# Two attention stages on one core: where the score maxima are subtracted, and when

## The chip, the cores and the metric

The kernel runs on one core of a Trainium2 chip. The metric is device time in microseconds (us), the median of the runs shown. A core has a matrix engine (PE, with its weight loads shown as PEld), a vector engine (DVE), an activation engine (ACT), GpSimd (POOL), and SyncE (SP), which here only issues DMAs. Each engine works through its own instructions in a fixed order; semaphores make one wait for another. PSUM is the memory into which PE writes.

## The reference

The input x is (8, 256, 512), cond is (8, 512), all float32. Four blocks are added to x one after the other. The change touches the first two, called here the masked and the modulated attention.

```python
# masked attention: x is (B, D, T), 8 heads of 32 channels, q = k = v
qh = (x^T @ Wq.T) in heads
logits = (scale * qh qh^T * cmask + (1 - cmask) * -1e30) * rmask
x = x + (softmax(logits) @ qh) @ Wo.T
# modulated attention: 16 heads of 32 channels
xn = rms_norm(x, g_norm) * (1 + scale) + shift     # scale, shift = cond @ W_emb + b_emb
q, k, v = xn @ W_qkv;  q = rms_norm(q, g_q);  k = rms_norm(k, g_k)
o = softmax(q k^T / sqrt(32)) @ v
x = x + o + o @ W_out
# then two scans over the 256 rows: an RK4 oscillator, and a GRU
```

## The kernel before

Attention and scans follow each other; the scans (from L540 on) keep eight batches together and walk through 256 steps. The attention part works on one batch at a time, with two stages interleaved by hand.

The order is written out: `for g in range(-5, ...)` walks over *slots*, and each slot calls small functions, each of which emits the instructions of one step. Instructions of one engine run in the order of these calls. Eight slots (`U = 8`) make a period, in which one batch passes through each step; `at(g, rel, n)` gives the batch and unit that a step serves in slot g. Below, "remainder r" means the slots with g mod 8 = r.

The masked stage has eight units per batch: two groups `e` of four heads, times four chunks `kc` of 128 keys. A unit is scored (`scores0`, L192) five slots before it is weighted (`weights0`, L224), and its values are summed (`values0`, L229) one slot later still. Scores are symmetric here, so the maximum over a row of a chunk (`maxima0`, L206) serves as maximum of a column. When the last chunk of a group is scored (remainders 3 and 7), `rows0` (L212) turns the maxima into a row, writes it to DRAM, and reads it back spread over 128 partitions into the tile `bc` (1 MB, one buffer). `weights0` subtracts `bc` on DVE (L226) from four heads' scores in SBUF, in one instruction of 128x2048, and ACT takes the exponential (L227). `weigh0` (remainders 1 and 5) divides on DVE, then masks and fills on POOL. `project`, `masked_out`, `normalize` and `modulate` come once or twice per period.

The modulated stage multiplies by `wqkv_sb` in six parts, one per slot (remainders 5, 6, 7, 0, 1, 2; two per slot for the last two batches). Of the q and k parts (remainders 7, 0, 1, 2) ACT makes squares and a copy, DVE sums (L326), POOL takes the power and scales (`qkv_norm`, L328 to L330), and one slot later PE transposes the result (`qkv_out`). Then come four groups `c` of four heads, one slot apart, from `HEADS[b]` on: `maxima1` in slot 0 of its own count, `rows1` and `weights1` in slot 1, `values1` in slot 2. `rows1` leaves the negative maxima as a row in SBUF; `weights1` forms the scores again with keys on the partitions and adds the row by a product with a column of ones (L384) into the same PSUM bank; ACT takes the exponential straight from PSUM.

All these steps take their PSUM banks from one pool of six, `ps_s`, in turn; a new bank waits until its last user, six banks ago, has been read. `values0` has two banks of its own, freed by `weigh0`.

At the end of slot 66 the masked stage's memory is closed and `follow()` issues the loads of the scan weights and of the transposed rows, all on SP (L535, L524), the queue which also carries the row and spread DMAs.

The names of the slots are those of the loop:

```python
            if a := at(g, 1, U):
                weights0(a[0], a[1] // 4, a[1] % 4)
...
            for part, lines in made:
                if lines:
                    qkv_norm(*part, *lines)
```

Of the kernel before, what the change touches and what calls it, by code (L numbers as in the profile page):

```python
# [14 lines left out]
P = 128  # L15
# [9 lines left out]
def attention(ctx, tc, cst, x, cond, wqT, woT, w_emb, b_emb, g_norm, w_qkv, g_q, g_k, w_out, follow):  # L25
# [53 lines left out]
    with tc.manual_schedule():  # L79
        nc.sync.dma_start(wq_sb, wqT.rearrange("(k p) e -> p k e", p=P))  # L80
        load(0)
        cst["rest"]()
        vec = wp.tile([12, P], F32, name="vec")
        nc.sync.dma_start(vec[0:8, :], b_emb.rearrange("(f p) -> f p", p=P))
        nc.sync.dma_start(vec[8:12, :], g_norm.rearrange("(f p) -> f p", p=P))
        gq_sb = wp.tile([P, 1], F32, name="gq_sb")
        gk_sb = wp.tile([P, 1], F32, name="gk_sb")
        for i in range(4):
            nc.sync.dma_start(gq_sb[32 * i : 32 * i + 32, :], g_q.unsqueeze(1))
            nc.sync.dma_start(gk_sb[32 * i : 32 * i + 32, :], g_k.unsqueeze(1))  # L90

        wemb = [
            two.tile([P, 2 * D], F32, tag=tag, name=f"wemb_{k}", bufs=bufs)
            for k, (tag, bufs) in enumerate((("qT", 1), ("kT", 1), ("vt", 2), ("vt", 2)))
        ]
        for k in range(NJ):
            nc.sync.dma_start(wemb[k], w_emb[k * P : (k + 1) * P, :])
        load(1)
        wo_sb = fone.tile([P, 2, 256], F32, name="wo_sb")
        nc.sync.dma_start(wo_sb, woT.rearrange("(k p) e -> p k e", p=P))  # L100
        wqkv_sb = wp.tile([P, NJ, 3 * D], F32, name="wqkv_sb")
        nc.sync.dma_start(wqkv_sb, w_qkv.rearrange("(k p) f -> p k f", p=P))
        wout_sb = wp.tile([P, NJ, D], F32, name="wout_sb")
        nc.sync.dma_start(wout_sb, w_out.rearrange("(k p) f -> p k f", p=P))

    gqs = wp.tile([P, 1], F32, name="gqs")
    mhalf = wp.tile([P, 16], F32, name="mhalf")
# [6 lines left out]
    mxp0 = [fone.tile([P, NJ, P], F32, name=f"mxp0_{i}") for i in range(2)]  # L114
    mxp1 = wp.tile([P, 2, P], F32, name="mxp1")
    for t in (*mxp0, mxp1):
# [6 lines left out]
    def modulation():  # L123

        nc.vector.tensor_scalar_mul(gqs, gq_sb, SC)
        pv = bank([P, 28], "pvs")
        nc.tensor.transpose(pv, cst["vecs"], ident[0:28, 0:28])
        nc.vector.tensor_copy(cst["vecS"], pv)
        pv = bank([P, 12], "pv")
        nc.tensor.transpose(pv, vec, ident[0:12, 0:12])  # L130
        nc.vector.tensor_copy(vecT, pv)
        pe = bank([P, 8, B], "pe")
        for f in range(8):
            for k in range(NJ):
                nc.tensor.matmul(
                    pe[:, f, :],
                    lhsT=wemb[k][:, f * P : (f + 1) * P],
                    rhs=condT[:, k, :],
                    start=(k == 0),
                    stop=(k == NJ - 1),  # L140
                )
# [3 lines left out]
        nc.vector.tensor_copy(shift, ssT[:, NJ:8, :])  # L145

        for c in range(NJ):
            nc.vector.tensor_add(wout_sb[:, c, c * P : (c + 1) * P], wout_sb[:, c, c * P : (c + 1) * P], ident)

# [19 lines left out]

    def project(b, e):  # L170
        if e == 0:
            qms[b] = ftwo.tile([P, 2, D], F32, tag="qm", name=f"qm_{b}")
# [6 lines left out]
        nc.vector.tensor_mul(qms[b][:, e, :], ps, mks[b])  # L179
# [11 lines left out]

    def scores0(b, e, kc):  # L192

        qm = qms[b]
        ss = [bank([P, D], f"s0_{b}_{e}_{kc}_{h}") for h in range(4)]
        for h in range(4):
            r = 32 * h
            nc.tensor.matmul(  # L198
                ss[h], lhsT=qm[r : r + 32, e, kc * P : (kc + 1) * P], rhs=qm[r : r + 32, e, :], start=True, stop=True
            )  # L200
        sc = ftwo.tile([P, 4, D], F32, tag="sc", name=f"sc_{b}_{e}_{kc}", bufs=7)
        for h in range(4):
            nc.scalar.copy(sc[:, h, :], ss[h])  # L203
        scs[b, e, kc] = sc

    def maxima0(b, e, qc):  # L206

        nc.vector.tensor_reduce(  # L208
            mxp0[e].rearrange("p q (h i) -> p q h i", i=32)[:, qc, :, 0], scs[b, e, qc], AX.X, ALU.max
        )  # L210

    def rows0(b, e):  # L212

        pt = bank([P, NJ, P], f"pm0_{b}_{e}")
        for qc in range(NJ):
            nc.tensor.transpose(pt[:, qc, :], mxp0[e][:, qc, :], ident)
        mrow = ftwo.tile([P, D], F32, tag="mrow", name=f"mrow0_{b}_{e}", bufs=1)
# [5 lines left out]

    def weights0(b, e, kc):  # L224
        sc = scs[b, e, kc]
        nc.vector.tensor_sub(sc, sc, bcs[b, e])  # L226
        nc.scalar.activation(sc, sc, AF.Exp, bias=negT[:, kc, b : b + 1], scale=SC)  # L227

    def values0(b, e, kc):  # L229
# [15 lines left out]

    def weigh0(b, e):

        fill = ftwo.tile([P, D], F32, tag="fill", name=f"fill_{b}_{e}", bufs=1)
        nc.gpsimd.tensor_scalar(fill, mks[b], -1.0, means[b, e], ALU.add, ALU.mult)
        cx = ctxTs[b][:, e, :]  # L250
        pv, pn = pc0s[b, e]
# [16 lines left out]
            nc.vector.tensor_add(xs[b][:, m, :], ps, xs[b][:, m, :])  # L268


    xhs, xnTs, qTs, kTs, vts, mrows1, exs1, oTs = {}, {}, {}, {}, {}, {}, {}, {}

    def normalize(b):
        ss = sm.tile([P, 2], F32, tag="ss", name=f"ss_{b}")
# [87 lines left out]
    def rows1(b, c):  # L362
        pt = bank([P, 2, P], f"pm1_{b}_{c}")
        for qc in range(2):
            nc.tensor.transpose(pt[:, qc, :], mxp1[:, qc, :], ident)
        mrows1[b, c] = two.tile([P, 256], F32, tag="mrow1", name=f"mrow1_{b}_{c}")
        nc.scalar.activation(mrows1[b, c], pt.rearrange("p q n -> p (q n)"), AF.Copy, scale=-1.0)

    def weights1(b, c):
        qT, kT, mrow = qTs[b], kTs[b], mrows1[b, c]  # L370
        ss = [bank([P, 2, 256], f"s1_{b}_{c}_{h}") for h in range(4)]
        for i in range(2):
            for h in range(4):
# [61 lines left out]
    for b in range(B):  # L435
# [26 lines left out]
    with tc.manual_schedule():  # L462
        for g in range(-5, OUT[-1][1] + 2):
# [549 lines left out]
```

## Time and profile before

| | |
|---|---|
| median of 3 runs | 2960.37 us (2959.13 to 2960.7) |
| the profiled execution, its own time | 2958.41 us |
| its span, from first to last instruction | 2956.6 us |
| mean granted clock of PE | 0.976 |
| PE, DVE, ACT, POOL busy, share of the span | 92%, 72%, 58%, 35% |
| first scan product (L709) on the chain of waits | 881.28 us |
| starts of slots 36, 44 and 52 (first `scores0` product) | 398.1, 497.1, 596.0 us |

The page's groups give for each line the engine, the operation, the tiles and shapes, the count, then busy time and mean length of one, then the idle time of the engine just before them and what ended it. A line of the timeline has the start in us, the length in us, the engine, the line and operation, and in brackets the wait before it. SPq is SyncE issuing DMAs; its length is the issue, not the transfer. A row of the windows has the stretch, its length, busy us and counts of PE, PEld, DVE, ACT, POOL, then the granted clock, the share of the DMA engines and GB/s. The spans of matmuls are modelled: where a matmul waits for a bank, its span may include the wait.

### The profile page before, as it was taken

To read this page: it belongs to the slowest core of one execution; us is meant where nothing else is said; L and a number is where in the kernel's file an instruction comes from. 1 tells how busy PE (TensorE), PEld (TensorE's weight loads), DVE (VectorE), ACT (ScalarE), POOL (GpSimd) and SP (SyncE) were. 2 spreads that over 40 slices of the span, in tenths; PEclk is the share of its full clock that TensorE was granted. 3 is DMA by queue.
4 is the path that set the end of the run, shared out by engine and by line. 5 is a ranking of instruction groups with operands and counts; after the bars stand their busy time and mean duration, and the time that the engine had idled before them with its cause. 6 is when DMAs were issued, how large, how long until landed. Compare 5 with 4: busy or idle time off the path is not lost.

```text
span 2956.6 us, 159809 instructions
## 1 busy us (share of the span) xinstructions
PE 2720.4 (92%) x67258; PEld 1930.5 (65%) x67258; DVE 2124.6 (72%) x8948; ACT 1720.9 (58%) x8427; POOL 1049.1 (35%) x2945
## 2 busy tenths in 40 slices
PE   6789999999988999999999999999999999999997
PEld 3234444444546777777777777777777777777776
DVE  4866676666446777777777777777777777777773
ACT  4655566554335666666666666666666666666551
POOL 0233123312313444444444444444444444444442
PEclk7989999999999999999999999999999999999998
DMA  3110101000600000000000000000000000000000
GB/s 143 40 40 29 40 26 47 29 33 23 129 15 4 7 6 7 6 7 7 7 6 7 6 7 7 6 6 7 7 7 7 6 7 7 6 7 6 6 7 6
DMA packets 27559, 57.60 MB, mean 19 GB/s; under 512 B 2816, under 2 KB 17164, under 8 KB 24788
## 3 DMA queue, kind: packets, MB, share of 16 engines
q1 hardware_dynamic: 26836, 47.36, 5.3%
q8 instruction: 526, 8.62, 1.2%
q14 instruction: 197, 1.61, 0.2%
HBM read 40.15 MB, written 7.21 MB: 16 GB/s over the span
## 4 chain that ended last, share of the span: by engine, by line
PE 39%; DVE 24%; ACT 5%; issue 3%; ACTq 0%; POOL 0%; DVEq 0%; POOLq 0%
PE pg L744 19%; PE ic L709 18%; DVE icT L901 5%; DVE qn L902 5%; ACT tT L609 4%; DVE hqs L862 3%; DVE own L759 3%; DVE sqmm L858 2%; DVE v L761 2%; DVE hz L789 2%; DVE own L778 1%; ACT sqmm L847 1%; DVE own L784 1%; PE psx L405 1%; ACTq L609 0%
## 5 line engine op out<-in xcount | busy, mean ns | idle before, releaser
L709 PE MATMUL ic<-cT_sb,tT 128*8 128x128 f32 x32736 | 1086.1, 273 | 82.3 <-ACT tT L609 45.6
L709 PEld LDWEIGHTS ic<-cT_sb,tT 128*8 128x8 f32 x32736 | 760.1, 89 | 339.8 <-ACT tT L609 268.5
L744 PE MATMUL pg<-whh_sb,hz 128*32 128x128 f32 x24576 | 820.9, 275 | 49.4 <-DVE hz L789 17.6
L609 ACT ACTIVATE tT<-qn 128x16 f32<-128x16 f32 x2046 | 440.8, 216 | 636.9 <-DVE qn L902 516.4
L744 PEld LDWEIGHTS pg<-whh_sb,hz 128*32 128x32 f32 x24576 | 669.5, 110 | 123.1 <-DVE hz L789 122.9
L901 DVE STREAM_TRANSPOSE icT<-ic 128x64 f32<-128x64 f32 x2048 | 504.2, 246 | 67.6 <-PE ic L709 63.2
L902 DVE SCALAR_TENSOR_TENSOR qn<-icT,hqs 128x16 f32<-128x16 f32 x2048 | 350.7, 171 | 70.1
L704 POOL TENSOR_TENSOR W<-W,cx 128x128 f32<-128x128 f32 x765 | 297.3, 389 | 256.6 <-ACT cx L690 256.4
L697 POOL TENSOR_TENSOR W<-cx,us 128x128 f32<-128x128 f32 x255 | 116.9, 458 | 445.0 <-ACT cx L690 445.0
L858 DVE SCALAR_TENSOR_TENSOR sqmm<-sqmm,qn 128x32 f32<-128x32 f32 x768 | 153.5, 200 | 151.4 <-ACT sqmm L847 122.4
L862 DVE TENSOR_TENSOR hqs<-W,sqmm 128x32 f32<-128x32 f32 x1020 | 199.9, 196 | 46.1 <-DVE own L784 1.0
L723 PE MATMUL gi<-wih_sb,x3T 128*32 128x384 f32 (+2 forms) x3072 | 201.5, 379 | 0.5 <-POOL x3T L914 0.5
L690 ACT ACTIVATE cx<-qn 128x32 f32<-128x32 f32 x1280 | 200.9, 213 | 0.0
L227 ACT ACTIVATE sc<-sc,negT 128x2048 f32<-128x2048 f32 x64 | 128.6, 2010 | 89.2 <-DVE sc L226 79.2
L305 PE MATMUL psqkv<-wqkv_sb,xnT 128*128 128x512 f32 x384 | 174.8, 600 | 0.2 <-DVE oT L165 0.2
L690 ACT ACTIVATE cx<-p 128x32 f32<-128x32 f32 x1020 | 149.8, 217 | 32.4 <-DVE p L857 1.6
L226 DVE TENSOR_TENSOR sc<-sc,bc 128x2048 f32<-128x2048 f32 x64 | 147.8, 2310 | 11.9 <-DMA bc<-row 11.9
L203 ACT COPY sc<-s 128x512 f32<-128x512 f32 x256 | 132.1, 617 | 40.6 <-PE s L198 40.4
L759 DVE STREAM_TRANSPOSE own<-pg 128x128 f32<-128x128 f32 x256 | 84.8, 331 | 94.8 <-PE pg L744 94.8
L208 DVE TENSOR_REDUCE mxp<-sc 128x4 f32<-128x2048 f32 x64 | 145.8, 2279 | 6.7 <-ACT sc L203 6.7
L690 ACT ACTIVATE cx<-q 128x32 f32<-128x32 f32 x1020 | 145.5, 213 | 0.0
L847 ACT ACTIVATE sqmm<-qn 128x32 f32<-128x32 f32 x768 | 140.5, 183 | 0.6
(149 smaller groups left out, 3364.0 us busy)
## 6 DMA issues: line engine op xcount, KB each, us to landing
bc<-row SPq DMA_DIRECT2D x16, 1024.0 KB
x<-in_x SPq DMA_DIRECT2D x8, 512.0 KB
out<-o SPq DMA_DIRECT2D x256, 16.0 KB
wqkv_sb<-in_L_cond_W_qkv SPq DMA_DIRECT2D x1, 3072.0 KB
wih_sb<-in_L_cond_W_ih SPq DMA_DIRECT2D x4, 768.0 KB
whh_sb<-in_L_cond_W_hh SPq DMA_DIRECT2D x4, 768.0 KB
x2d<-x2o SPq DMA_DIRECT2D x11, 256.0 KB
x2T<-x2d SPq DMA_DIRECT2D x11, 256.0 KB
```

Source lines behind the costliest of these rows:

```text
L305: nc.tensor.matmul(ps, lhsT=xnTs[b][:, c, m * P : (m + 1) * P], rhs=wqkv_sb[:, c, part * D : (part + 1) * D], start=(c == 0), stop=(c == N ...
L609: nc.scalar.activation(tT, src[:, half * HM : (half + 1) * HM, :], AF.Tanh)
L690: nc.scalar.activation(c[:, i], x, AF.Copy, scale=f)
L704: nc.gpsimd.tensor_tensor(W[:, i + 1 : 5], W[:, i + 1 : 5], c, ALU.add)
L709: nc.tensor.matmul(ps[32 * j : 32 * j + B, :], lhsT=tT[k // HM][:, k % HM, :], rhs=cT_sb[:, k, j * P : (j + 1) * P], start=(k == 0), stop= ...
L723: nc.tensor.matmul(gi_ps[rows(j), g0:g1, :], lhsT=x3T[c][:, k, :], rhs=wih_sb[:, k, g0:g1, j * P : (j + 1) * P], start=(k == 0), stop=(k = ...
L744: nc.tensor.matmul(pg_ps[rows(j), :], lhsT=hzs[tau % 3][:, k, 32 * g : 32 * g + 32], rhs=whh_sb[:, k, g, j * P : (j + 1) * P], start=((k, ...
L759: nc.vector.transpose(pgt.rearrange("p m n -> p (m n)"), pg_ps)
L858: stt(mm, sq, LIN[s], qs, ALU.subtract, ALU.mult)
L862: nc.vector.tensor_sub(hq, W[:, s], mm)
L901: nc.vector.transpose(icT.rearrange("p m n -> p (m n)"), ic[:, half * 64 : half * 64 + 64])
L902: stt(qn[:, m2, :], icT[:, :, 0:B], IC[s], hq[:, m2, :], ALU.mult, ALU.add)
```

## The change

- `weights0` subtracts on GpSimd (POOL) instead of DVE.
- `rows1` writes the maxima to DRAM and reads them back spread over 128 partitions (`bc1`, 512 KB, two buffers). `weights1` drops the product with ones; DVE subtracts `bc1` from the scores in PSUM, ACT takes the exponential of the result in SBUF.
- The heads' steps lie one slot further apart from their maxima: `weights1` two slots after `maxima1`, `values1` three. Within a slot both stand ahead of `qkv_out` and `qkv_norm`. `modulated_out` comes 8 and 9 slots after `HEADS[b]` instead of 6 and 8 (7 and 8 instead of 6 and 7 for the last two batches), so the loop has one slot more.
- `rows0` stands right behind the last `maxima0` instead of at the slot's end. There is one `mxp0` tile instead of two; `mrow` and `fill` share a buffer; `qm` is one tile per head group.
- `modulation()` runs in slot 1 instead of 4; the identity is added to `wout_sb` in slot 8; `w_qkv` and `w_out` are loaded at the end of slot -1 instead of ahead of the loop.

```diff
-        wqkv_sb = wp.tile([P, NJ, 3 * D], F32, name="wqkv_sb")
+    wqkv_sb = wp.tile([P, NJ, 3 * D], F32, name="wqkv_sb")
+    wout_sb = wp.tile([P, NJ, D], F32, name="wout_sb")
+
+    def load_weights():
+
         nc.sync.dma_start(wqkv_sb, w_qkv.rearrange("(k p) f -> p k f", p=P))
-        wout_sb = wp.tile([P, NJ, D], F32, name="wout_sb")
         nc.sync.dma_start(wout_sb, w_out.rearrange("(k p) f -> p k f", p=P))
...
     def weights0(b, e, kc):
         sc = scs[b, e, kc]
-        nc.vector.tensor_sub(sc, sc, bcs[b, e])
+        nc.gpsimd.tensor_tensor(sc, sc, bcs[b, e], ALU.subtract)
         nc.scalar.activation(sc, sc, AF.Exp, bias=negT[:, kc, b : b + 1], scale=SC)
...
-        mrows1[b, c] = two.tile([P, 256], F32, tag="mrow1", name=f"mrow1_{b}_{c}")
-        nc.scalar.activation(mrows1[b, c], pt.rearrange("p q n -> p (q n)"), AF.Copy, scale=-1.0)
+        mrow = two.tile([P, 256], F32, tag="mrow1", name=f"mrow1_{b}_{c}")
+        nc.scalar.copy(mrow, pt.rearrange("p q n -> p (q n)"))
+        row = dram.tile([4, 256], F32, tag="row1", name=f"row1_{b}_{c}", bufs=2)
+        nc.sync.dma_start(row, mrow.rearrange("(h i) n -> h i n", i=32)[:, 0, :])
+        bc = bcs1[b, c] = two.tile([P, 4, 256], F32, tag="bc1", name=f"bc1_{b}_{c}")
+        nc.sync.dma_start(bc, row.rearrange("h n -> (h n)").partition_broadcast(P).rearrange("p (h n) -> p h n", h=4))
...
                     start=True,
-                    stop=False,
-                )
-            for h in range(4):
-                r = 32 * h
-                nc.tensor.matmul(
-                    ss[h][:, i, :], lhsT=ones[r : r + 1, :], rhs=mrow[r : r + 1, :], start=False, stop=True
+                    stop=True,
                 )
...
             ex = sm.tile([P, 2, 256], F32, tag="ex1", name=f"ex1_{b}_{c}_{h}", bufs=4)
-            nc.scalar.activation(ex, ss[h], AF.Exp)
+            nc.vector.tensor_sub(ex, ss[h], bc[:, h, :].unsqueeze(1).to_broadcast([P, 2, 256]))
+            nc.scalar.activation(ex, ex, AF.Exp)
...
-        OUT.append((HEADS[b] + 6, HEADS[b] + (8 if per == 1 else 7)))
+        OUT.append((HEADS[b] + (8 if per == 1 else 7), HEADS[b] + (9 if per == 1 else 8)))
...
-            if g == 4:
+            if g == 1:
                 modulation()
+            if g == U:
+                add_identity()
...
-            for a in leave("qkv"):
-                qkv_out(*a)
             for b in range(B):
                 if g in OUT[b]:
                     m = OUT[b].index(g)
                     left["x2", b, m] = modulated_out(b, m)
+
+            if a := heads(g, 3):
+                values1(*a)
+            if a := heads(g, 2):
+                weights1(*a)
+            for a in leave("qkv"):
+                qkv_out(*a)
...
             if last:
                 maxima0(a[0], a[1] // 4, 3)
+                rows0(a[0], a[1] // 4)
             if a1:
                 maxima1(*a1)
-            if a2 := heads(g, 2):
-                values1(*a2)
-            if a2 := heads(g, 1):
-                weights1(*a2)
             if a and not last:
                 maxima0(a[0], a[1] // 4, a[1] % 4)
-            if last:
-                rows0(a[0], a[1] // 4)
             if (a2 := at(g, -7)) and a2[0] > 1:
                 load(a2[0])
+            if g == -1:
+                load_weights()
```

More of the change, by code (lines that the diff above doesn't have):

```diff
@@ L113, in attention @@
     nc.vector.tensor_scalar(negT, condT, NEG, -NEG, ALU.mult, ALU.add)
-    mxp0 = [fone.tile([P, NJ, P], F32, name=f"mxp0_{i}") for i in range(2)]
+    mxp0 = fone.tile([P, NJ, P], F32, name="mxp0")
     mxp1 = wp.tile([P, 2, P], F32, name="mxp1")
-    for t in (*mxp0, mxp1):
+    for t in (mxp0, mxp1):
         nc.vector.memset(t, 0.0)
@@ L145, in modulation, with add_identity @@
         nc.vector.tensor_copy(shift, ssT[:, NJ:8, :])
+    def add_identity():
         for c in range(NJ):
@@ L171, in project @@
         if e == 0:
-            qms[b] = ftwo.tile([P, 2, D], F32, tag="qm", name=f"qm_{b}")
             qtoks[b] = ftwo.tile([P, NJ, 256], F32, tag="qtok", name=f"qtok_{b}")
@@ L178, in project @@
             )
-        nc.vector.tensor_mul(qms[b][:, e, :], ps, mks[b])
+        qms[b, e] = ftwo.tile([P, D], F32, tag="qm", name=f"qm_{b}_{e}", bufs=3)
+        nc.vector.tensor_mul(qms[b, e], ps, mks[b])
         qt = line(f"qt_{b}_{e}")
@@ L192, in scores0 @@
     def scores0(b, e, kc):
-        qm = qms[b]
+        qm = qms[b, e]
         ss = [bank([P, D], f"s0_{b}_{e}_{kc}_{h}") for h in range(4)]
@@ L198, in scores0 @@
             nc.tensor.matmul(
-                ss[h], lhsT=qm[r : r + 32, e, kc * P : (kc + 1) * P], rhs=qm[r : r + 32, e, :], start=True, stop=True
+                ss[h], lhsT=qm[r : r + 32, kc * P : (kc + 1) * P], rhs=qm[r : r + 32, :], start=True, stop=True
             )
@@ L208, in maxima0 @@
         nc.vector.tensor_reduce(
-            mxp0[e].rearrange("p q (h i) -> p q h i", i=32)[:, qc, :, 0], scs[b, e, qc], AX.X, ALU.max
+            mxp0.rearrange("p q (h i) -> p q h i", i=32)[:, qc, :, 0], scs[b, e, qc], AX.X, ALU.max
         )
@@ L215, in rows0 @@
         for qc in range(NJ):
-            nc.tensor.transpose(pt[:, qc, :], mxp0[e][:, qc, :], ident)
-        mrow = ftwo.tile([P, D], F32, tag="mrow", name=f"mrow0_{b}_{e}", bufs=1)
+            nc.tensor.transpose(pt[:, qc, :], mxp0[:, qc, :], ident)
+        mrow = ftwo.tile([P, D], F32, tag="row", name=f"mrow0_{b}_{e}", bufs=1)
         nc.scalar.copy(mrow, pt.rearrange("p q n -> p (q n)"))
@@ L246, in weigh0 @@
     def weigh0(b, e):
-        fill = ftwo.tile([P, D], F32, tag="fill", name=f"fill_{b}_{e}", bufs=1)
+        fill = ftwo.tile([P, D], F32, tag="row", name=f"fill_{b}_{e}", bufs=1)
         nc.gpsimd.tensor_scalar(fill, mks[b], -1.0, means[b, e], ALU.add, ALU.mult)
@@ L268, in masked_out @@
             nc.vector.tensor_add(xs[b][:, m, :], ps, xs[b][:, m, :])
-    xhs, xnTs, qTs, kTs, vts, mrows1, exs1, oTs = {}, {}, {}, {}, {}, {}, {}, {}
+    xhs, xnTs, qTs, kTs, vts, bcs1, exs1, oTs = {}, {}, {}, {}, {}, {}, {}, {}
     def normalize(b):
@@ L365, in rows1 @@
             nc.tensor.transpose(pt[:, qc, :], mxp1[:, qc, :], ident)
-        mrows1[b, c] = two.tile([P, 256], F32, tag="mrow1", name=f"mrow1_{b}_{c}")
-        nc.scalar.activation(mrows1[b, c], pt.rearrange("p q n -> p (q n)"), AF.Copy, scale=-1.0)
+        mrow = two.tile([P, 256], F32, tag="mrow1", name=f"mrow1_{b}_{c}")
[4 more added lines that the diff above has]
+        nc.sync.dma_start(bc, row.rearrange("h n -> (h n)").partition_broadcast(P).rearrange("p (h n) -> p h n", h=4))
     def weights1(b, c):
-        qT, kT, mrow = qTs[b], kTs[b], mrows1[b, c]
+        qT, kT, bc = qTs[b], kTs[b], bcs1[b, c]
         ss = [bank([P, 2, 256], f"s1_{b}_{c}_{h}") for h in range(4)]
```

## The prediction, written before the changed kernel ran

> **What bounds the kernel now.** I read the page first, then the chain of waits, the windows of the attention stage, its timeline slot by slot, and at the end SyncE's own timeline.
>
> ```profile
> PE 2720.4 (92%) x67258; PEld 1930.5 (65%) x67258; DVE 2124.6 (72%) x8948; ACT 1720.9 (58%) x8427; POOL 1049.1 (35%) x2945
> ...
> PE pg L744 19%; PE ic L709 18%; DVE icT L901 5%; DVE qn L902 5%; ACT tT L609 4%; DVE hqs L862 3%; DVE own L759 3%; DVE sqmm L858 2%; DVE v L761 2%; DVE hz L789 2%; DVE own L778 1%; ACT sqmm L847 1%; DVE own L784 1%; PE psx L405 1%; ACTq L609 0%
> ...
> L226 DVE TENSOR_TENSOR sc<-sc,bc 128x2048 f32<-128x2048 f32 x64 | 147.8, 2310 | 11.9 <-DMA bc<-row 11.9
> ...
> L704 POOL TENSOR_TENSOR W<-W,cx 128x128 f32<-128x128 f32 x765 | 297.3, 389 | 256.6 <-ACT cx L690 256.4
> ```
>
> The chain is nearly all scan (L709, L744). The scans start at 881 us and are not touched, so the change moves the time by what it does to the 881 us before them. There eight slots make a period of 99 us (slot 36 starts at 398.1, slot 44 at 497.1, slot 52 at 596.0).
>
> ```profile
> 400.00:450.00 50.00, 48.62 (x421) 24.88 (x420) 35.75 (x32) 28.87 (x49) 6.19 (x6) 0.97 0.09 27
> 450.00:500.00 50.00, 46.10 (x244) 18.11 (x245) 33.75 (x29) 29.89 (x49) 19.18 (x17) 0.97 0.13 43
> ```
>
> The columns are PE, PEld, DVE, ACT, POOL busy, clock, DMA. PE looks 95% busy, but that hides waits inside a matmul's span: eight L198 stream in 0.86 us when free, yet take 2.1 to 3.3 us where they wait for PSUM banks. Added up from free-running rows (0.43 us for a 128x512 pass), a period holds 78 us of PE work of 99. So the stage is bound by hand-overs in the fixed order of each engine, not by one engine's work. The timeline of slot 39 (it starts at 437.73) shows the one that matters:
>
> ```profile
> 446.39 0.69 DVE L326 TENSOR_REDUCE s<-sq 128x16 f32<-128x512 f32 x1 [3.28 <-ACT sq L318]
> ...
> 447.17 0.20 POOL L328 TENSOR_SCALAR r<-s 128x16 f32<-128x16 f32 x1 [25.78 <-DVE s L326]
> 447.46 2.93 POOL L329 TENSOR_TENSOR r<-r,mhalf 128x16 f32<-128x16 f32 x1
> ...
> 450.47 1.05 POOL L330 TENSOR_TENSOR qr<-qr,r 128x512 f32<-128x512 f32 x1
> ```
>
> POOL needs 4.4 us (447.17 to 451.52) for one q/k normalisation, in four slots of eight (remainders 7, 0, 1, 2), and nothing else stands behind it there.
>
> **POOL subtraction.** 64 DVE subtractions of 2.31 us go (147.8 us), 64 POOL ones come. Price: POOL two-input rows are 389 ns at 128x128 (L704) and 1274 ns at 128x512 (L257), so 2.305 ns a column and 1274 + 1536 x 2.305 = 4.81 us. Low end 4 x 1.05 = 4.2 us (L330, one input repeated); high end 6.7 us, from a POOL fill that took 2.60 instead of 0.69 us beside DVE. I take 4.81, nearest to L257. POOL rises by 308 us, to some 64 us of a period: enough room.
>
> The Trainium skill ("GPSIMD Engine Reference", the elementwise comparison) speaks against this step: it gives 4497 ns on GpSimd and 2293 ns on VectorE for a two-input add of this width; with its figure the loop below would be 0.3 us shorter per slot.
>
> Does DVE hold POOL up? It does today:
>
> ```profile
> 178.49 2.28 DVE L226 TENSOR_TENSOR sc<-sc,bc 128x2048 f32<-128x2048 f32 x1
> 178.60 2.24 POOL L328 TENSOR_SCALAR r<-s 128x16 f32<-128x16 f32 x1
> ```
>
> A 0.20 us instruction lasts until L226 ends. L226 is the only DVE operation of the stage with both inputs in SBUF, and it goes; beside PSUM-reading L410 (472.96) POOL's L257 kept its 1.28 us. So no surcharge.
>
> **What queues behind it.** In each slot the exponential of the masked scores (L227, 2.0 us) waits for the subtraction, and behind it on ACT stand that slot's L318/L320, the modulated exponentials, L344 and the next score copies. On POOL the subtraction of slot g+1 stands behind the normalisation of slot g, which needs DVE's sum L326, which needs ACT's L318 of slot g, which stands behind the exponential of slot g. That closes a loop in the normalising slots: normalise 4.4 + subtract 4.85 + exponential 2.05 + square 0.6 + sum 0.75 = 12.65 us per slot. In between slots POOL runs ahead, so remainder 7 enters free. Counted from its start to the start of remainder 4:
> - sum of squares done after 14.4 us: scores with bank waits 1.9, values 1.7, q/k products 3.4, `values1` 1.8, DVE reciprocal and multiply 2.2, four new subtractions 2.75, sum 0.7 (before: 447.08 - 437.73 = 9.4, since the sum came ahead of these);
> - to the next sum 16.2: PE meets `rows0` right behind `maxima0` of DVE and stands until 17.2, then 7.8 us to the end of `values1` and 5.65 us of DVE;
> - two loops, 25.3; the last normalisation 4.4;
> - remainder 3: subtract 4.85, exponential 2.05, L182 0.8, squares 1.6, scale 1.0, L282 1.4, L344 0.7, `maxima1` 0.9 = 13.3.
>
> Sum 73.6 us against 497.07 - 437.73 = 59.3: +14. The other three slots (39.6 us) lose about 2 us by the part below. So +12 a period, for five periods (slots 20 to 60) **+60 us**. My same hand sum for the old order gives 90 of its 99 us, so +20 is possible; if POOL ran further ahead than I see, +4. The first batch alone (slots 15 to 20, no heads): first sum at 7.4, then 37.9 + 4.4 + 13.3 = 63 against 199.8 - 145.7 = 54.1, **+9** (4 to 12). The two doubled slots of batch 6, two normalisations (8.7) ahead of the last subtraction: **+8** (0 to 12).
>
> **Maxima spread by DRAM.** Gone: the L384 products, 0.43 us for four heads, twice for each of 32 groups, 28 us of PE, and PE's wait for L367 in the same slot. Where the loop bounds, that buys nothing; elsewhere it is the 2 us above. New: 128 DVE subtractions of 128x512 from PSUM at 0.69 (L410), 88 us, and 32 row writes and 512 KB spreads on SP. A row lands in 1.75 us (452.40 to 454.14); a 1 MB spread takes 4.7 us, so 3.5 for half (2.4 to 4.7). A slot covers that in the middle. At the end nothing does: copy 0.4, row 1.75, spread 3.5, subtract and exponential 3.3 make 9 us per group against 6.0 to 6.6 (`values1` at 854.62, 860.87, 866.92), three times and a partly covered first: +10. The last batch's sums now stand behind reciprocals and subtractions, +9; its output product moves out of their way, -4. **+15** (5 to 22).
>
> **SP's queue.** The scan loads are issued at the end of slot 66; `rows1` of batch 6, groups 1 to 3, come behind them.
>
> ```profile
> 770.07 1.82 SPq L535 DMA_DIRECT2D cT_sb<-in_L_cond_coupling  x4
> ...
> 773.91 3.31 SPq L535 DMA_DIRECT2D whh_sb<-in_L_cond_W_hh  x4
> 781.49 31.99 SPq L524 DMA_DIRECT2D x2T<-x2d  x11
> ```
> ```profile
> 796.00:800.00 4.00, 4.00 (x18) 1.86 (x21) 0.00 (x0) 1.13 (x3) 0.00 (x0) 1.00 1.03 218
> ```
>
> SP is occupied until 813.5, and the DMA share stays at 1.0 until 817. Group 1's spread then lands near 821; its subtractions, in slot 68, would be due at 803. DVE waits, behind it the maxima of group 3, which hold PE's banks: **+19** (5 to 25).
>
> **Start.** Today 4 MB of weights stand ahead of the first row:
>
> ```profile
> 32.99 0.35 SPq L222 DMA_DIRECT2D bc<-row  x1
> 37.72 2.29 DVE L226 TENSOR_TENSOR sc<-sc,bc 128x2048 f32<-128x2048 f32 x1 [7.33 <-DMA bc<-row]
> ...
> 42.16 1.94 PE L238 MATMUL pc<-sc,qtok 128*32 128x512 f32 x8 [10.98 <-ACT sc L227]
> ...
> 59.37 6.97 PE L135 MATMUL pe<-condT,wemb 128*128 128x8 f32 x47
> ```
>
> With the weights behind it the row (24.63) lands at 26.4 and the spread at 31.1, 6.6 us earlier. The modulation's 10.5 us of PE (59.4 to 69.9) fall into the 11 us in which PE waits; without that cover they would cost what they cost now. DVE's maxima of unit 5 queue behind them until about 38, and ran at 39.9 before. Then POOL sets the pace: four subtractions 19.3, the single `bc` buffer refilled 4.7, fill and two context steps 3.2, 27.2 us for four slots against 26 (L226 of unit 4 at 73.67, unit 8 at 99.47). Subtractions begin 18.6, 17 and 24 us earlier (units 4, 8, 12) and last 2.5 longer: **-18** (-12 to -22). The identity add (0.9 us) and shared row buffers cost nothing: their users are two slots apart.
>
> **Sum.** -18 + 9 + 60 + 8 + 19 + 15 = +93. The profiled run has its own 2958.41 us (span 2956.6), 1.96 under the median of 2960.37; 2958.4 + 93 + 2 = 3053 us. All low ends together give +12 (2972), all high ends +159 (3119).
>
> **Rivals.**
> - Faster (0.11): PE's order is what ends last and the loop is covered. For: PE shows 95%, the loop closes only in four slots. Against: PE waits of 21 us a period. Price: the period scales with PE work, 78.2 less 3.5 for L384, 99 x 74.7/78.2 = 94.6, so -4.4, five times -22, start -18, tail and SP +10: 2930. It decides if the ACT exponential finds its input ready in remainders 0 to 3, which needs a POOL subtraction of about 2 us, or a loop below the 10.5 us that slots 40 to 42 take now.
> - Loop hidden, but SP jam and tail in full (0.04): -40 + 34, 2955, no change.
> - POOL is also blocked by DVE's PSUM-reading work (0.05): 6.7 us each, 1.9 more in four links, 7.6 a period, five times +38: 3091, and more where the first batch and the start feel it too.
>
> The Trainium skill ("SBUF — State Buffer", the shared port pair) says a DVE instruction with two SBUF inputs excludes a GpSimd one that reads SBUF; the two rows at 178.5 agree. By that page this last rival would not happen.
>
> **How the numbers follow.** My forecast has 0.80, and 3053 is its time. The range 2970 to 3110 reaches from all low ends to near all high ends, takes in most of the third rival, and leaves out the faster one and the upper tail. A measurement of this kernel can tell about 0.2% (6 us) from no change. Faster 0.11, same 0.03, slower 0.86.
>
> **What would show it.** Right: POOL subtraction near 4.8 us x64; in remainders 0 to 3 ACT's exponential waiting for POOL by 5 us and more; a period near 111 us; DVE waiting for the modulated spread once for some 15 us near the scan loads; the first masked values near 38. Wrong: a period of 99 or less, that exponential never waiting, or that spread arriving ahead of the scan loads.

## The result, and the profile after

The changed kernel takes 3143.44 us (median of 4 runs, 3140.49 to 3145.13) against 2960.14 us for the kernel before (4 runs, 2959.13 to 2960.7): 1.062 times as long, 95% interval 1.0603 to 1.0637, +183 us. Predicted were 3053 us (+93) and at most 3110: the sign was right, the size half of what came; even all high ends of the prediction's terms together (3119) lie below the result. The profiled execution of after took 3144.8 us.

| stretch, from the starts of the slots | before | after | difference | predicted |
|---|---|---|---|---|
| start to slot 20 | 199.8 | 203.5 | +4 | -9 (-18 and +9) |
| slots 20 to 52, four periods | 396.2 | 490.2 | +94 | +48 |
| slot 52 to the end, a period more, batches 6 and 7 | 2362.4 | 2451.1 | +89 | +54 (12, 8, 19, 15) |

These are the two profiled executions, 3144.8 less 2958.4 = +186.

Line numbers are those of each kernel's own file: in the changed one `weights0` is L232 and L233, `values0` L244, `qkv` L311, `qkv_norm` L332 to L336, `maxima1` L358 and L366, `weights1` L385 to L396, the reciprocal behind `values1` L170, the scan loads L545 and L534.

The page after, first the engines, then groups as explained above (busy and mean, then the idle time of the engine just before them):

```profile
PE 2801.5 (89%) x66746; PEld 1935.9 (62%) x66746; DVE 2067.1 (66%) x9011; ACT 1731.5 (55%) x8427; POOL 1324.2 (42%) x3009
...
L232 POOL TENSOR_TENSOR sc<-sc,bc 128x2048 f32<-128x2048 f32 x64 | 289.0, 4524 | 28.7 <-DMA bc<-row 28.7
...
L233 ACT ACTIVATE sc<-sc,negT 128x2048 f32<-128x2048 f32 x64 | 128.5, 2008 | 180.9 <-POOL sc L232 180.8
...
L396 ACT ACTIVATE ex<-ex 128x512 f32<-128x512 f32 x128 | 77.5, 630 | 147.9 <-DVE ex L395 147.9
```

PE is busy 81 us longer for 512 matmuls fewer. ACT's masked exponential (L233) now waits 180.9 us for POOL, ACT's modulated one (L396) 147.9 us for DVE. The windows of one period, slots 36 to 44 (PE, PEld, DVE, ACT, POOL busy, granted clock, DMA share, GB/s), of after and then of before:

```profile
447.97:569.79 121.82, 106.92 (x589) 44.21 (x585) 61.03 (x66) 59.60 (x94) 60.33 (x31) 0.86 0.13 46
```
```profile
398.11:497.07 98.96, 93.67 (x649) 42.66 (x648) 68.46 (x59) 57.73 (x94) 25.37 (x22) 0.97 0.11 36
```

121.8 us instead of 99.0, DVE and POOL each only half busy, and PE's clock at 0.86 instead of 0.97. Slot 39 of after (490.34 to 511.52), which the prediction followed, and the beginning of slot 40:

```profile
493.74 1.94 PE L244 MATMUL pc<-sc,qtok 128*32 128x512 f32 x8
...
497.31 4.42 PE L311 MATMUL psqkv<-wqkv_sb,xnT 128*128 128x512 f32 x8
...
503.66 1.76 DVE L170 RECIPROCAL r<-pc 128x256 f32<-128x256 f32 x1 [8.49 <-PE pc L160]
...
505.80 2.47 DVE L395 TENSOR_TENSOR ex<-s,bc 128x512 f32<-128x512 f32 x4
...
508.19 0.68 DVE L332 TENSOR_REDUCE s<-sq 128x16 f32<-128x512 f32 x1
...
508.95 0.20 POOL L334 TENSOR_SCALAR r<-s 128x16 f32<-128x16 f32 x1 [25.04 <-DVE s L332]
...
511.12 0.47 PE L222 MATMUL pm<-ident,mxp 128*128 128x128 f32 x1 [4.57 <-DVE mxp L214]
...
513.26 4.53 POOL L232 TENSOR_TENSOR sc<-sc,bc 128x2048 f32<-128x2048 f32 x1
...
517.83 2.00 ACT L233 ACTIVATE sc<-sc,negT 128x2048 f32<-128x2048 f32 x1 [2.14 <-POOL sc L232]
```

Read down: the sum L332 stands behind reciprocal and four subtractions on DVE, POOL waits 25 us for it, its masked subtraction stands behind the normalisation, and ACT waits for that. In slots 40 to 43 that last wait is 2.1, 6.3, 7.9 and 6.6 us. So the loop is there. What the prediction had too small comes before it: the first sum ends 18.5 us into slot 39, not 14.4.

### The profile page after: what moved, and what is told of

It reads as the page before. It is cut to its first block, busy times and chain, and to the rows that moved or that the text cites. A ratio compares the mean times of both kernels' runs of the same rounds, so it can differ in the third digit from the quotient of the medians.

```text
span 3143.0 us, 159050 instructions
## 1 busy us (share of the span) xinstructions
PE 2801.5 (89%) x66746; PEld 1935.9 (62%) x66746; DVE 2067.1 (66%) x9011; ACT 1731.5 (55%) x8427; POOL 1324.2 (42%) x3009
## 4 chain that ended last, share of the span: by engine, by line
PE 53%; DVE 26%; ACT 7%; POOL 6%; issue 4%; DMA 2%; SPq 1%; ACTq 0%; DVEq 0%; POOLq 0%
PE pg L754 18%; PE ic L719 16%; DVE icT L911 5%; DVE qn L912 4%; PE psqkv L311 4%; ACT tT L619 4%; PE pc L244 4%; DVE hqs L872 3%; POOL sc L232 3%; PE s L204 3%; DVE own L769 3%; DVE sqmm L868 2%; DVE v L771 2%; PE n L358 2%; POOL r L335 2%
## 5 line engine op out<-in xcount | busy, mean ns | idle before, releaser
L232 POOL TENSOR_TENSOR sc<-sc,bc 128x2048 f32<-128x2048 f32 x64 | 289.0, 4524 | 28.7 <-DMA bc<-row 28.7
L233 ACT ACTIVATE sc<-sc,negT 128x2048 f32<-128x2048 f32 x64 | 128.5, 2008 | 180.9 <-POOL sc L232 180.8
L311 PE MATMUL psqkv<-wqkv_sb,xnT 128*128 128x512 f32 x384 | 180.0, 615 | 1.0 <-DVE oT L171 1.0
L170 DVE RECIPROCAL r<-pc 128x256 f32<-128x256 f32 x32 | 56.2, 1758 | 186.5 <-PE pc L160 186.5
L396 ACT ACTIVATE ex<-ex 128x512 f32<-128x512 f32 x128 | 77.5, 630 | 147.9 <-DVE ex L395 147.9
L204 PE MATMUL s<-qm 32*128 32x512 f32 x512 | 143.1, 798 | 14.6 <-ACT qr L326 8.9
```

What stands on the lines that cost most here:

```text
L204: nc.tensor.matmul(ss[h], lhsT=qm[r : r + 32, kc * P : (kc + 1) * P], rhs=qm[r : r + 32, :], start=True, stop=True)
L232: nc.gpsimd.tensor_tensor(sc, sc, bcs[b, e], ALU.subtract)
L311: nc.tensor.matmul(ps, lhsT=xnTs[b][:, c, m * P : (m + 1) * P], rhs=wqkv_sb[:, c, part * D : (part + 1) * D], start=(c == 0), stop=(c == N ...
```

## The experiments

Each run has its ratio to the kernel before with a 95% interval. A period is read from the starts of the slots, as above.

### Which part costs what: two switches

**e1: masked subtraction back on DVE.**
```diff
-        nc.gpsimd.tensor_tensor(sc, sc, bcs[b, e], ALU.subtract)
+        nc.vector.tensor_sub(sc, sc, bcs[b, e])
```


> The changed kernel with one line put back: the masked maxima are subtracted on DVE again. Loop theory (subtraction behind normalisation on POOL, exponential behind the subtraction on ACT, squares behind the exponential, closes a ring): the stretch from a remainder-7 slot to the next remainder 4, 79.5 us in the changed kernel, falls to about 60, the period from 122 to about 101, the time to 3143 - 5 x 21 - 15 = about 3025. Rival, order and banks (modulated scores now wait in PSUM for DVE, the maxima of the next group stand right behind them and wait for the same banks, PE's granted clock sinks to 0.8): with 2.3 us more on DVE in each slot the period stays at 115 or more, the time at 3110 or more.

3083.57 us, ratio 1.0412 (1.0385 to 1.0439): 60 us less than the changed kernel, between the two expectations. Periods are 112.6 to 116 us. Two thirds of the loss have nothing to do with POOL.

**e9: e1, without the subtraction of the modulated maxima.**
```diff
-            nc.vector.tensor_sub(ex, ss[h], bc[:, h, :].unsqueeze(1).to_broadcast([P, 2, 256]))
-            nc.scalar.activation(ex, ex, AF.Exp)
+            nc.scalar.activation(ex, ss[h], AF.Exp)
```


> The changed kernel with the subtraction back on DVE, and without the subtraction of the modulated maxima (left out; ACT takes the exponential straight from PSUM, the spread is made and not read). It takes 88 us of DVE work away and leaves the order as it is. If these instructions on DVE's queue are the price of the new order: period 100 to 104, and no DVE wait for the spread at the scan loads, 3000 to 3025 us. If the order costs by itself: period 110 or more, only the wait at the scan loads goes (some 28 us), 3050 to 3060 us.

2965.38 us, ratio 1.0034 (1.0017 to 1.0051), lower than either expected. What is left of the change here (new order, longer distance, start moves, 64 more DMAs, no products with ones) costs 0.3% net; taking 128 DVE instructions of 0.68 us (79 us of busy time, since they overlap a little) out of e1 buys 118 us. Not all of that lies in the periods. From the traces of e1 and e9: 51 us between slots 20 and 52, 20 from there to the first product of batch 6's maxima, 35 from that one to batch 7's (the stretch of the scan loads, where DVE in e1 waits for a spread that e9 does not read), 12 behind, and 4 the other way at the start.

**e11: the changed kernel, POOL and all, with the same edit as e9.**

> The changed kernel with its subtraction on GpSimd, without the subtraction of the modulated maxima (left out; exponential straight from PSUM). It asks whether the two costs add. If they do: 3143 less 118 (what these instructions cost with the masked subtraction on DVE) is 3025 us, or 2965 plus the 44 that GpSimd's subtraction cost in the kernel before, 3010 us: 3005 to 3030 us, periods 107 to 112. Rival: GpSimd's loop paces the slots by itself, so that leaving out DVE work buys little: above 3070 us, periods 116 and more.

3015.62 us, ratio 1.0194 (1.0179 to 1.0209), as expected if the costs add. With the changed kernel this makes a square:

| time in us (slots 36 to 44, granted clock there) | masked subtraction on DVE | on POOL | POOL costs |
|---|---|---|---|
| modulated maxima not subtracted | 2965 (102.5, 0.93) | 3016 (109.3, 0.94) | +50 |
| subtracted on DVE from PSUM | 3084 (112.6, 0.89) | 3143 (121.8, 0.86) | +60 |
| the subtractions cost | +118 | +128 | |

**e2: the kernel before, with only the masked subtraction on POOL.**

> The kernel before with one line changed: the masked maxima are subtracted on POOL. Loop theory: three loops of about 12.4 us (subtraction 4.52 as measured) enter the stretch from remainder 7 to remainder 4, first sum at 9.4 as before: 9.4 + 37 + 4.4 + 12.4 = 63 against 59.3, so +4 a period, +20 in five, +8 in the first batch and the start a few us slower, about 2990 to 3010. Rival, order and banks: DVE is freed of 2.3 us a slot and nothing else moves, 2950 to 2965.

3003.42 us, ratio 1.0148 (1.0128 to 1.0167), +44: 19 us by slot 20, then 6 to 8 us in each period (105 to 107 us). The loop theory's range held it.

### Is POOL's price the loop?

**e3: the changed kernel with `qkv_norm` ahead of the heads' steps.** DVE's sum L332 comes ahead of reciprocal and subtractions.
```diff
+            turned = list(leave("qkv"))
+            for part, lines in made:
+                if lines:
+                    qkv_norm(*part, *lines)
+                    left["qkv", *part] = lines[1]
             if a := heads(g, 3):
                 values1(*a)
             if a := heads(g, 2):
                 weights1(*a)
-            for a in leave("qkv"):
+            for a in turned:
                 qkv_out(*a)
-            for part, lines in made:
...
```


> The changed kernel with the q/k sums and normalisation called ahead of values1 and weights1 in each slot, so that DVE sums before it divides and subtracts. Loop theory with its place of entry: the first sum is done about 8 us sooner after the slot begins (18.5 to about 10.5), the second link falls from 18.6 to about 13, 13 us a period, time about 3143 - 65 = 3075. Rival, order and banks: the sums are not on the path, 3130 to 3150.

3093.23 us, ratio 1.0456 (1.0437 to 1.0475), -50, where 68 had been expected. Between 195 and 700 us ACT's masked exponential waits 62 us for POOL, in the changed kernel 96.

**e14: the same move, with the masked subtraction on DVE.**

> The changed kernel with the masked subtraction back on DVE (3083.6 us) and the normalisation of q and k ahead of the heads' values and weights. On the changed kernel itself that move alone bought 50 us. If it did so by shortening GpSimd's loop, it is worth within 12 us of nothing here: 3072 to 3096 us. Rival: it did so by moving DVE's sum ahead of the reciprocal and the new subtractions, whoever subtracts the masked maxima: 3030 to 3050 us.

3092.2 us, ratio 1.0446 (1.0431 to 1.0462), +9 against e1 (the granted clock in slots 36 to 44 is 0.83 here, 0.89 in e1; why, was not followed). With the sum ahead, POOL and DVE as subtracter differ by 1 us (ratios 1.0456 and 1.0446), with the sum behind by 60. So POOL's price is the loop (subtraction behind normalisation, sum behind subtractions, square behind exponential), not its 4.5 us as such; that PE's slower rows hide a part of it in e3 and e14 is not excluded.

### Why do the subtractions from PSUM cost more than they last?

The same slot (38) in e1 and in e9, here from the products of `weights1` on. e1:

```profile
463.72 1.15 PE L385 MATMUL s<-qT,kT 32*128 32x256 f32 x16
463.86 1.76 DVE L170 RECIPROCAL r<-pc 128x256 f32<-128x256 f32 x1 [6.47 <-PE pc L160]
...
465.99 2.47 DVE L395 TENSOR_TENSOR ex<-s,bc 128x512 f32<-128x512 f32 x4
466.22 2.61 PE L358 MATMUL n<-kT,qT 32*128 32x256 f32 x15 [0.99 <-DVE oT L171]
...
468.67 2.48 DVE L366 TENSOR_REDUCE mxp<-n 128x2 f32<-128x512 f32 x4 [0.21 <-PE n L358]
...
472.01 1.94 PE L244 MATMUL pc<-sc,qtok 128*32 128x512 f32 x8
```

e9, where ACT empties the banks of `weights1` itself:

```profile
434.79 1.15 PE L385 MATMUL s<-qT,kT 32*128 32x256 f32 x16
...
436.01 2.06 ACT L395 ACTIVATE ex<-s 128x512 f32<-128x512 f32 x4 [1.58 <-PE s L385]
...
437.30 1.26 PE L358 MATMUL n<-kT,qT 32*128 32x256 f32 x15 [0.99 <-DVE oT L171]
...
440.82 1.06 PE L244 MATMUL pc<-sc,qtok 128*32 128x512 f32 x8
```

From these products to the next masked values PE takes 8.3 us in e1 and 6.0 in e9. Six banks go round, so `maxima1` (L358) gets banks that `weights1` had, and those are emptied by DVE, behind its reciprocal; then the next masked scores get banks of `maxima1`, emptied by DVE again. PE stands between DVE instructions twice. This is read from the order and the waits; no run changes the banks alone. And PE's next rows are slow: 1.94 us instead of 1.06 for the masked values, which lie in slot 39 (granted clock 0.77 there in e1, 0.95 in e9). In slot 38 itself it is

```profile
450.26:468.52 18.26, 17.27 (x104) 7.50 (x99) 11.44 (x12) 7.11 (x12) 0.00 (x0) 0.76 0.09 30
```

in e1, against

```profile
424.84:438.23 13.39, 12.40 (x103) 5.72 (x100) 9.06 (x8) 7.03 (x12) 1.77 (x2) 1.00 0.12 39
```

in e9. Whether the clock is part of the price or only goes along with it, added PE work can tell: `weights1` writes the same scores several times more into the bank that DVE reads last, so PE works where it would wait.
```diff
+        for _ in range(N):
+            nc.tensor.matmul(
+                ss[3][:, 1, :], lhsT=kT[96:128, c, P : 2 * P], rhs=qT[96:128, c, :], start=True, stop=True
+            )
```
**e13: N = 24.** 

> The changed kernel with the masked subtraction back on DVE (3083.6 us), and 24 more products of 32x128 by 32x256 in each head group, which write the same scores again into the bank that DVE subtracts from last: PE works 1.7 us longer where it would wait for DVE. If the low granted clock behind that wait is half of the price (values 3.6 us instead of 1.9, q/k/v product 4.0 to 4.5 instead of 3.7 in the same slot without the subtractions), the clock stays up and the period falls by 4 to 8 us: 3040 to 3065 us. Rival: the clock does not come back, or the added products only lengthen PE's work: 3085 to 3135 us.

3516.84 us, ratio 1.1884 (1.1864 to 1.1903), far off both. I had reckoned 0.07 us for one, from the 16 matmuls over four heads that take 1.15 us in L385; but the record has two matmuls for each product, and the added ones, all on the same 32 rows of the array and all into the same half of a bank, took far longer each:

```profile
558.54 15.18 PE L393 MATMUL s<-qT,kT 32*128 32x256 f32 x48
...
578.81 1.06 PE L244 MATMUL pc<-sc,qtok 128*32 128x512 f32 x8
```

15.18 us for 24 products (48 matmuls), 0.63 each. But the masked values behind them were at full speed again.

**e15: N = 3.** 

> As the run with 24 added products per head group, but with 3 of them: there each took 0.63 us at the granted clock of 0.7, eight times what I had reckoned, so that 3 fill 1.3 to 1.9 us, the time in which PE waits for DVE. In that run the rows of the slot behind the filler were at full speed again (values 1.06 us instead of 1.93, q/k/v product 3.70 instead of 4.50). If the slow rows are half of the price, and come from PE's waits: period down by 4 to 8 us from 114, 3045 to 3068 us. Rival: the clock does not come back with so little, or the filler lengthens PE's path by as much as it gains: 3075 to 3120 us.

3071.19 us, ratio 1.0388 (1.0342 to 1.0434). The filler takes 1.45 us; masked values at 1.94 us as before. It leans neither way.

**e17: N = 6.** 

> As the run with 3 added products per head group (3071 us, 12 below the kernel without them; they took 1.45 us, and the slow rows stayed), with 6: 2.9 us, still done before DVE comes to the last of the four banks (4.0 us behind the scores). If PE's low clock behind its waits is a large part of the price, the rows behind are at full speed now (values 1.06 us, not 1.94) and the time falls further, to 3035 to 3060 us. Rival: the clock does not follow, or the stretch is set by DVE's own chain: 3065 to 3085 us.

3051.42 us, ratio 1.0311 (1.0296 to 1.0327), 32 us less than e1 (30 by the two ratios) with 88 us more of PE work. The same slot (38):

```profile
447.61 2.75 PE L393 MATMUL s<-qT,kT 32*128 32x256 f32 x12
...
454.22 1.07 PE L244 MATMUL pc<-sc,qtok 128*32 128x512 f32 x8
```

Full speed again, the slot 14.9 us instead of 18.3, the periods from slot 28 on 106 us instead of 112.6 to 116. Added products can only lengthen PE's queue, so what is gained comes from its faster rows: at least some 30 of the 118 us are PE's low clock, and here it comes back when the wait for DVE is filled.

**e18: N = 10.** 

> The same with 10 added products, 4.8 us, 0.8 us more than DVE's chain gives. If the clock is a large part: rows at full speed, time within 15 us of the run with 6, the lengthened chain eating some of the gain: 3040 to 3075 us. Rival: each added product now costs its own time, 16 times 0.8 and more: 3090 to 3130 us.

3139.83 us, ratio 1.0593 (1.0555 to 1.0632), above both ranges: 88 us more than with 6. The four more products in 32 head groups are 61 us by themselves (0.48 each). In slot 38 the clock is 1.00 as with 6, but over slots 20 to 52 it is 0.87 (0.94 with 6, 0.87 in e1), and a matmul of the masked values takes 778 ns on average over the attention (704 with 6). Past the wait that is there, the filler is path. Why the clock falls in other slots again, and why 3 products did not raise it in this one, stays open.

### Is it the order within the slot?

**e7: e1 with the order of before (transposes of q and k ahead, heads behind the maxima, row of masked maxima at the slot's end).** 

> The changed kernel with the subtraction back on DVE (3083.6 us, periods 112.6 to 116) and with the order within a slot as it was before: transposes of q and k ahead, values and weights of the heads behind the maxima, the row of masked maxima at the slot's end. The spread, the DVE subtractions from PSUM and the longer distance stay. Order theory (steps stand in the wrong place for DVE's queue): the period falls to 100 to 104, about -55, 3020 to 3035 us. Rival (88 us more of DVE work and later bank release cost wherever they stand): period 110 or more, 3060 us or above.

3039.73 us, ratio 1.0283 (1.0244 to 1.0321): between the two. Periods of 107.5 to 112 us; 18 of the 44 us come between slots 20 and 52, 28 behind, and 3 are lost ahead. So the order is worth 44 us; most of the price of the subtractions stays wherever they stand.

**e8: e1 with only the row of masked maxima back at the slot's end.** 

> The changed kernel with the subtraction back on DVE, and only the row of masked maxima back at the slot's end. If PE standing at its transposes for DVE's last maximum (4.6 us twice a period) is what counts, the period falls by 5 to 9 us, 3035 to 3055 us. If the heads' place ahead of the normalisation counts, little changes: 3075 to 3090 us.

3089.91 us, ratio 1.045 (1.0417 to 1.0483), 6 us more than e1. But the run does not settle its question: the 4.57 us wait at L222 stands once in a period, in remainder 7, where no maxima of heads follow and the edit moves nothing, and e8 still has it. What went is a wait of 2.28 us in remainder 3, and that bought nothing. What the longer wait costs was not tested.

### The end and the start

In the changed kernel SyncE is held by the loads of the scans, and DVE waits for the spread behind them:

```profile
928.35 30.35 SPq L534 DMA_DIRECT2D x2T<-x2d  x10
...
967.00 2.48 DVE L395 TENSOR_TENSOR ex<-s,bc 128x512 f32<-128x512 f32 x4 [29.42 <-DMA bc<-row]
```

**e4: the changed kernel with the scan loads three slots later (slot 69).** 

> The changed kernel with the scan weights and transposed rows loaded at the end of slot 69 instead of 66, so that the spreads of batch 6 stand ahead of them on SP. SP theory: the one wait of DVE for a spread, 29.4 us, goes, and the loads still end before the scans begin: 3143 - 27 = about 3116. Rival: 47 us of full DMA engines now meet the spreads of batch 7 and delay those instead, 3135 to 3150.

3134.10 us, ratio 1.059 (1.0574 to 1.0606), only 9 us less. The loads then jammed batch 7's spread (DVE waited 22.7 us there), as the rival said, 1 us below its range.

**e16: e1, the two DMAs of the modulated spread issued by POOL.** 

> The changed kernel with the masked subtraction back on DVE (3083.6 us, where DVE waits 28 us for the modulated spread at the scan loads), and the two DMAs of each modulated spread issued by GpSimd instead of SyncE. If SyncE's queue alone holds the spread up, that wait goes and with it 25 to 34 us: 3050 to 3060 us. If the transfers themselves are held up, because the scan loads keep the DMA engines busy, the wait stays above 15 us: 3070 us or more.

```profile
833.22 2.48 DVE L395 TENSOR_TENSOR ex<-s,bc 128x512 f32<-128x512 f32 x4 [7.71 <-DMA bc<-row]
...
872.87 2.48 DVE L395 TENSOR_TENSOR ex<-s,bc 128x512 f32<-128x512 f32 x4 [9.09 <-DMA bc<-row]
...
928.16 2.48 DVE L395 TENSOR_TENSOR ex<-s,bc 128x512 f32<-128x512 f32 x4 [8.17 <-DMA bc<-row]
```

3085.93 us, ratio 1.0436 (1.0396 to 1.0476), no gain on e1. The wait at the loads fell from 28.4 to 9.1 us, so SyncE's queue was most of it, but the time did not follow as either ending had it: two other spreads now wait, since POOL issues their rows only behind two normalisations, and DVE waits 7.7 and 8.2 us for them. From the first product of batch 6's maxima to that of batch 7's it is 95 us, 107 in e1, 72 in e9 and 73 in e11; the 12 us won there are lost ahead of it (8 us) and behind it (4 us).

**e5: the kernel before with only the moves of the start.** 

> The kernel before with only the moves of the start: modulation in slot 1, identity in slot 8, the loads of the two modulated weights at the end of slot -1. My prediction's start term (row 24.6, spread landing at 31 instead of 37.7) then stands alone, with the subtraction still on DVE: 2940 to 2950 us, slot 20 near 186 to 190 instead of 199.8. Rival: the modulation's products and the first batch's other waits take the place of that wait, and slot 20 stays within 3 us of 199.8: 2955 to 2965 us.

2955.32 us (10 runs) against 2958.89, ratio 0.9999 (0.9982 to 1.0016): nothing. Slot 20 starts at 198.0, before at 199.8.

```profile
32.73 13.82 PE L138 MATMUL pe<-condT,wemb 128*128 128x8 f32 x64
34.75 2.29 DVE L231 TENSOR_TENSOR sc<-sc,bc 128x2048 f32<-128x2048 f32 x1 [0.77 <-DMA bc<-row]
```

The spread lands in time for DVE at 34.8, but PE is in the modulation from 32.7 to 46.5 (13.8 us; in the kernel before 10.6).

### A faster version

**e12: the kernel before without the modulated maxima.** It rests on q and k being normalised, so that the scores stay bounded as long as the gains `g_q` and `g_k` are moderate.
```diff
-            if a := heads(g, 1):
-                rows1(*a)
...
-            if a1:
-                maxima1(*a1)
...
-                nc.tensor.matmul(
-                    ss[h][:, i, :], lhsT=ones[r : r + 1, :], rhs=mrow[r : r + 1, :], start=False, stop=True
-                )
```


> The kernel before, without the modulated maxima, their rows and the product with ones (left out: the exponential is taken of the plain scores, which normalised q and k keep bounded). The runs point to the modulated maxima as the dear part. PE loses some 10 us a period (16 products four times, products with ones, transposes), DVE 10 us of maxima. If the modulated side paces the slots: period 88 to 93, 2905 to 2935 us. Rival: the masked side paces them: period 96 or more, 2945 us or above.

2876.68 us, ratio 0.9725 (0.9709 to 0.9741), 82 us faster than the kernel before and faster than I had expected. The periods are 88.6 to 93.3 us, as expected, and the scans start at 803.4 us instead of 881.3, so that 78 us of the gain lie ahead of them.

## Why the prediction was half right

- **POOL's subtraction and its loop: right.** 4.52 us measured for 4.81 (the figure in the Trainium skill, "GPSIMD Engine Reference", the elementwise comparison, 4497 ns, was nearer than my row). In my sum the loop had +32 in the periods (12 less two links of 2.75, five times), +9 for the first batch and +8 in batch 6: +50 with roundings. The square gives +50 to +60, e2 +44; between the traces of e1 and of the changed kernel it is +12 by slot 20 (predicted 9), +33 in the four periods (26) and +12 from slot 52 to the scans (14). Two loops took 25.5 us (25.3), the last normalisation 4.4 (4.4), remainder 3 12.4 (13.3).
- **"New: 128 DVE subtractions of 128x512 from PSUM at 0.69 (L410), 88 us": the step that failed.** Their length was right (0.68). I priced them at 2.75 us in two links of the loop, 27 us in five periods, and at 34 us of tail and jam, some 61 in all. They cost 118 to 128 (square); with the masked subtraction on DVE 51 us of it lie in four periods, where the sum had 22, and 35 around the scan loads, where it had 19. What I missed is what they do to PE: the traces show them holding the banks that PE needs next, behind a reciprocal, in the slots with heads, and e17 shows PE's clock falling behind such waits as some 30 us of the price. How the rest divides between the waits and the order (e7: 44 us) no run separates. "Gone: the L384 products ... elsewhere it is the 2 us above" shows no gain: in e9, which has neither product nor subtraction, the periods are 98.6 to 102.8 us, not below 99 as a rule.
- **First sum 14.4, measured 18.5; second link (from that sum to the next) 16.2, measured 18.6.** In the first sum DVE's terms were right: reciprocal and multiply 2.1 us (2.2), subtractions 2.4 (2.75), sum 0.7 (0.7). All of the 4.1 us are PE's terms: scores 3.4 us instead of 1.9, values 3.6 instead of 1.7, q/k products 4.35 instead of 3.4, `values1` 2.0 instead of 1.8. I summed PE's rows at their free-running lengths. In slot 39 of the kernel before the clock is 1.00:

```profile
440.17 1.06 PE L238 MATMUL pc<-sc,qtok 128*32 128x512 f32 x8
...
442.03 3.70 PE L305 MATMUL psqkv<-wqkv_sb,xnT 128*128 128x512 f32 x8
```

  In the changed kernel it is 0.78 in that slot, and the same rows take 1.94 and 4.42 us. The 0.86 us for eight free L198 was too low as well; the fastest in the trace take 1.14. The three slots without normalisation grew by 2.8 us and did not lose 2. That is slot 36 (15.1 us instead of 11.8), which is as long in e11 and e9 (15.1, 15.3) but 12.7 in e1, which has the same order; what sets it stays open.
- **Start, "-18": wrong; 2 us of it came in e5, 8 in e1 (whose first row went out at 24.7 us, e5's at 28.2), and POOL's first batch took more than that back: slot 20 at 203.5 us, in e1 at 191.6.** I let the modulation hide in an 11 us wait that the same edit removed. With the row early there was no wait left to cover 13.8 us of PE. First masked values came at 47.4, not 38.
- **Jam, "+19", and tail, "+15".** DVE waited 29.4 us, and the stretch between the maxima of batches 6 and 7 grew by 35; from batch 7's first maxima to the scans it was +10, and +38 from slot 52 to batch 6's first maxima (predicted 12 and 8). The mechanism was there, its size was off. e16 confirms that SyncE's queue was most of the long wait, though taking the spreads off it won nothing in the end.
- **Rivals.** The faster one did not happen, nor the one with the loop hidden: ACT's exponential does wait for POOL. The time lies beyond the rival in which DVE blocks POOL (3091 and more), but not by its mechanism: POOL's subtraction took 4.52 us on average in all five kernels that have it there.

## What to carry to other kernels

Price an instruction that reads PSUM by what its engine does ahead of it and by who needs the bank next, not by its length: 79 us of DVE work cost 118, a part of it because they also made DVE wait for a DMA. Take PE's rows from a stretch with the same waits: the same row can take nearly twice as long behind one. An idle engine is no free engine if its queue closes a loop with the others: with one 0.7 us sum moved ahead, POOL instead of DVE cost 1 us and no longer 60. And a wait that an edit removes cannot at the same time be the cover for work that the edit moves into it.

## What the hardware showed unexpectedly

- PE at little more than half speed behind waits of a few us: the same eight matmuls took 1.94 us and 1.06 us, and 6 useless products (2.75 us) in the wait made the kernel 32 us faster, while 3 left those rows slow. The Trainium skill ("TensorE: Matmul & The Clock Gate", "A second HAM failure mode: psum-queue depth-cycling") describes a kernel whose PE idles briefly between groups while it cycles through banks, so that the clock gate swings between half and full rate; e17 agrees, with a granted clock of 0.76 in slot 38 of e1 and 1.00 with the filler.
- Products of 32 rows ran side by side where they stood on different rows of the array: 16 matmuls over four row groups took 1.15 us (0.07 each), 48 in one row group 15.18 (0.32 each, at a granted clock of 0.69 meanwhile). Those 48 also wrote the same half of one bank; which of the two counts, no run separates.
- Ten loads of 256 KB held SyncE for 30.35 us of issuing. The Trainium skill ("DMA: Bandwidth & Descriptors", "Issuing engines are not separate DMA queues") says that another issuing engine saves only the time that the sequencer takes to start a DMA, usually small beside the DMA; here it took the wait at the loads from 28.4 to 9.1 us, and nothing off the total.
